# Cross attention's probabilities: two of four tiles turned by VectorE and through DRAM

## The chip, the cores and the metric

The kernel runs on one core of a Trainium2 chip. A core has a matrix engine, TensorE (PE in the profile; PEld is its weight load), and three others that compute: VectorE (DVE), ScalarE (ACT) and GpSimd (POOL). SyncE (SP) computes nothing; here it issues every DMA, in the order in which the program lists them, and when one has to wait, the ones behind it wait too. Each engine works through a list of its own, and semaphores make it wait for others. SBUF is the on-chip memory of 128 partitions, PSUM the eight banks into which TensorE writes, DRAM the large memory outside. The metric is the device time of one execution in microseconds. Lower is better.

## The reference

An encoder and a decoder layer of a transformer, in float32. The source has 2 x 77 tokens, the target 2 x 2048, the model 512 features, 16 heads of 32, and a feed-forward width of 2048. The part in question is the decoder's cross attention, then its feed-forward:

```python
def _mha(xq, xkv, w_in, b_in, w_out, b_out, bias):
    q = (xq @ wq.T + bq).reshape(Bq, Tq, H, hd).transpose(0, 2, 1, 3)
    ...
    scores = jnp.einsum('bhqd,bhkd->bhqk', q, k) / jnp.sqrt(hd) + bias[None]
    attn = jax.nn.softmax(scores, axis=-1)
    out = jnp.einsum('bhqk,bhkd->bhqd', attn, v).transpose(0, 2, 1, 3).reshape(Bq, Tq, D)
    return out @ w_out.T + b_out
...
y = y + _mha(yn, yn, ..., sb)                      # self attention, causal
y = y + _mha(_ln(y, ...), memory, ..., cb)         # cross attention: 77 keys
h = _ln(y, ...)
y = y + (jax.nn.relu(h @ dec_ff1_w.T + dec_ff1_b) @ dec_ff2_w.T + dec_ff2_b)
```

The bias depends on the distance of key and query, cut off at 127; against 77 keys it differs from head to head by a constant only from the third tile of 128 queries on, which the softmax does not see. So only the first two tiles of each batch have a bias added.

## The kernel before

The target is cut into 8 blocks of 512 tokens (2 batches of 4), a block into 4 tiles of 128 tokens. The first part of the program, up to about 1665 us, is self attention, with the encoder and the first block's cross attention woven in. The second part runs the feed-forward of block x and, between its matmuls, the cross attention of block x + 1, so seven times in all.

A block of the second part has 56 slots. Slots 0 to 27 each run one product of the first feed-forward matmul (L1636), slots 28 to 55 two products of the second (L1665; every fourth slot has one). Both are done by a scheme that multiplies seven products of halves instead of eight, so partial sums stay in a PSUM bank and go on being added to after an engine has read them: a bank that has been read late holds up a matmul four slots on. The stages of cross attention are functions which a table puts into slots; in a slot they are issued first, then the slot's own products, then the DMAs of the next weight tiles (`feed`, L1548). For tile t the table was: scores at slot 13 + 5t, and the others 2, 3, 3, 7 and 11 slots on.

The stages of one tile:

- **score**: 16 products of a head's queries with the 77 keys (L822; the queries lie in a buffer called `bias`, the keys in `pts`), into four banks. VectorE adds the bias where there is one (L829), takes each row's maximum (L831) and subtracts it on the way into SBUF (L832). The destination `pr` has 16 x 77 columns; tiles 0 and 2 use a part of the tile named `oT`, tiles 1 and 3 a part of `pts`.
- **exp**: ScalarE, one instruction over `pr` (L835).
- **sums**: VectorE sums each head's row and takes the reciprocal (L840, L841).
- **normalize**: GpSimd multiplies `pr` by it (L846).
- **turned**: TensorE turns each head's 128 x 77 into 77 x 128, four heads to a bank, and ScalarE copies each bank to `pts` (L852, L853).
- **times_v**: 16 products with v, four heads beside one another on the array (L860), and a copy by ScalarE (L864).

After each second tile come the out-projection's products (L1799, added by VectorE at L1803) in `O_SLOTS`, slots 31 to 34 and 40 to 43, and then each tile's normalization for the feed-forward (L779 to L800). Evictions of the first feed-forward matmul are L1646, L1649 and L1652, those of the second L1673 to L1685; the sums of halves that it needs are L1585, L1603 and L948.

Weight tiles of 256 KB come through a ring of 16 in `pp`. When a slot's products are done with a tile, SP loads the tile that will be used 16 tiles later into its place. Residual rows (`vv<-y`, L1359) and output rows (L1693) go through the same SP queue. A DMA on this queue uses one of eight semaphores in turn.

## Time and profile before

| | |
|---|---|
| time, median of 3 runs | 2706.46 us (2704.81 to 2711.2) |
| the profiled execution | 2708.39 us, its span 2706.3 us, granted clock 0.998 |
| PE, PEld, DVE, ACT, POOL busy | 99%, 81%, 68%, 56%, 37% of the span |
| second part, 1670 to 2606 us: PE, DVE, ACT, POOL busy | 936.0, 530.1, 388.8, 520.7 us of 936 |
| DMA in that stretch | 0.65 of the 16 engines, 195 GB/s |

Times are in us from the start of the span, unless marked ns. A group's row reads: line, engine, operation, output<-inputs with shapes, count | busy time, mean ns of one | idle time of the engine just before them and what ended it. A row of the chain of waits has start, length, and what ran. A row of a timeline has start, length, engine, line and instruction. A float32 product shows as two rows on PE, a turn as one: 16 products with v are "x32", 16 turns "x16".

### The profile page before, as it was taken

Reading aid. Unit: us, or ns where it says so; the run is one execution under the profiler, and the core shown is the slowest. Engines: PE = TensorE matmul, PEld = TensorE weight load, DVE = VectorE, ACT = ScalarE, POOL = GpSimd, SP = SyncE. Lnnn points to the kernel's source line nnn. Section 1 sums busy time; section 2 is a strip of 40 time slices with the busy share of each in tenths; the row PEclk is TensorE's granted clock in tenths of the full one; section 3 lists DMA queues with packets and bytes.
Section 4 is the critical chain, followed back from the end, with each engine's and each line's share of the span. In section 5 each row is a group of like instructions: output and inputs, shape, how many; then the busy total and the mean of one; then the engine's idle time right before and its main releaser. Section 6 shows DMA issues by size and latency. Waiting matters only on the chain.

```text
span 2706.3 us, 68257 instructions
## 1 busy us (share of the span) xinstructions
PE 2684.3 (99%) x26606; PEld 2199.2 (81%) x26606; DVE 1848.9 (68%) x5448; ACT 1526.2 (56%) x2960; POOL 1002.3 (37%) x844
## 2 busy tenths in 40 slices
PE   9999999999999999999999999999999999999998
PEld 6678777777776677778777887999999898989898
DVE  4776688888885687788888883737464746464635
ACT  3545567767886557777767794444443444444431
POOL 2602235500300513223300103556565555556546
PEclk9999999999999999999999999999999999999999
DMA  8734445511213522343311216565658565657575
GB/s 235 215 99 131 128 146 174 169 59 43 64 49 87 144 80 81 111 126 118 107 53 40 73 59 196 176 211 172 215 169 241 172 215 171 215 170 216 153 222 186
DMA packets 296276, 385.10 MB, mean 142 GB/s; under 512 B 41184, under 2 KB 165648, under 8 KB 295826
## 3 DMA queue, kind: packets, MB, share of 16 engines
q1 hardware_dynamic: 295954, 380.73, 46.9%
q8 instruction: 211, 3.46, 0.5%
q14 instruction: 111, 0.91, 0.1%
HBM read 334.15 MB, written 46.47 MB: 141 GB/s over the span
## 4 chain that ended last, share of the span: by engine, by line
PE 96%; DVE 1%; ACT 1%; DMA 1%; POOL 1%; SPq 0%; issue 0%; DVEq 0%; POOLq 0%; ACTq 0%
PE psum L417 18%; PE psum L1636 15%; PE psum L1665 13%; PE psum L375 11%; PE psum L441 9%; PE psum L1120 8%; PE psum L1799 3%; PE psum L1756 3%; PE psum L1035 3%; PE psum L852 2%; PE psum L822 1%; PE psum L860 1%; PE psum L576 1%; PE psum L797 1%; PE psum L239 1%; PE psum L215 1%
## 5 line engine op out<-in xcount | busy, mean ns | idle before, releaser
L406 ACT ACTIVATE pp<-pp,nm 128x128 f32<-128x128 f32 (+15 forms) x512 | 611.4, 1200 | 23.4 <-DVE nm L401 23.2
L384 DVE TENSOR_SCALAR_CACHE_REDUCE pp<-psum 128x512 f32<-128x512 f32 (+3 forms) x1024 | 556.7, 590 | 69.2 <-PE psum L375 67.1
L423 ACT COPY pts<-psum 128x512 f32<-128x512 f32 x696 | 374.4, 593 | 346.3 <-PE psum L417 309.5
L417 PE MATMUL psum<-ident,pp 128*128 128x128 f32 x4352 | 527.4, 276 | 5.7 <-ACT nT L310 4.0
L417 PEld LDWEIGHTS psum<-ident,pp 128*128 128x128 f32 x4352 | 475.2, 141 | 64.5 <-issue 21.4
L441 PEld LDWEIGHTS psum<-pts,vv 128*32 128x32 f32 x8704 | 225.7, 110 | 119.4 <-DVE pp L384 49.3
L375 PE MATMUL psum<-kT,q 32*128 32x512 f32 (+3 forms) x2560 | 320.3, 565 | 2.2 <-ACT kT L231 1.4
L421 DVE COPY pts<-psum 128x512 f32<-128x512 f32 x392 | 257.7, 686 | 84.8 <-PE psum L417 81.3
L1665 PE MATMUL psum<-pp 128*128 128x128 f32 x2560 | 304.5, 276 | 1.9 <-POOL pp L948 1.6
L1665 PEld LDWEIGHTS psum<-pp 128*128 128x128 f32 x2560 | 296.3, 192 | 8.6 <-issue 2.8
L441 PE MATMUL psum<-pts,vv 128*32 128x128 f32 x8704 | 278.0, 275 | 1.1 <-DVE pp L384 0.8
L948 POOL TENSOR_TENSOR pp<-pp 128x512 f32<-128x512 f32 x159 | 212.8, 1355 | 110.2 <-ACT pp L800 45.4
L1636 PE MATMUL psum<-vv,pp 128*128 128x256 f32 x1024 | 236.2, 381 | 0.0
L1636 PEld LDWEIGHTS psum<-vv,pp 128*128 128x128 f32 x1024 | 190.3, 190 | 25.8 <-issue 0.5
L391 DVE CUSTOM_DVE_ANT_0 pp<-psum,bias 128x256 f32<-128x256 f32 (+1 forms) x512 | 196.0, 411 | 13.2 <-PE psum L375 12.7
L375 PEld LDWEIGHTS psum<-kT,q 32*128 32x128 f32 x2560 | 127.5, 183 | 87.3 <-issue 50.0
L1649 DVE TENSOR_TENSOR kT<-kT,psum 128x512 f32<-128x512 f32 x96 | 65.8, 686 | 191.1 <-PE psum L1636 190.9
L1652 ACT ACTIVATE kT<-kT,vecs 128x256 f32<-128x256 f32 x192 | 86.9, 501 | 156.6 <-DVE kT L1649 155.9
L1636 PE MATMUL psum<-nT,pp 128*128 128x256 f32 x768 | 174.1, 380 | 0.0
L1636 PEld LDWEIGHTS psum<-nT,pp 128*128 128x128 f32 x768 | 144.2, 190 | 20.3 <-issue 1.6
L1673 ACT COPY oT<-psum 128x128 f32<-128x128 f32 x56 | 15.0, 268 | 239.1 <-PE psum L1665 239.1
L480 POOL TENSOR_TENSOR oT<-rirows,oT 128x512 f32<-128x512 f32 x30 | 38.4, 1279 | 288.6 <-DMA rirows<-rec 267.0
(272 smaller groups left out, 4108.2 us busy)
## 6 DMA issues: line engine op xcount, KB each, us to landing
pp<-w_d SPq DMA_DIRECT2D x520, 256.0 KB
pp<-in_dec_ff_wT_dram SPq DMA_DIRECT2D x112, 256.0 KB
bias<-tzg SPq DMA_DIRECT2D x128, 128.0 KB
pp<-wo_d SPq DMA_DIRECT2D x56, 256.0 KB
wqk<-in_dec_sa_in_wT_dram SPq DMA_DIRECT2D x52, 256.0 KB
wqk<-sa_q SPq DMA_DIRECT2D x84, 128.0 KB
vv<-in_enc_ff_wT_dram SPq DMA_DIRECT2D x8, 1024.0 KB
xr<-in_x_dram SPq DMA_DIRECT2D x32, 256.0 KB
```

Source lines behind the costliest of these rows:

```text
L375: nc.tensor.matmul(banks[r][:, : kn * P], q[rows4(r), ts(t, P)], kT[rows4(r), g, k0 * P : (k0 + kn) * P], start=True, stop=True,)
L384: nc.vector.tensor_scalar(p[:, k0 : k0 + far], s[:, :far], 1.0, None, ALU.mult, ALU.max, accum_out=st["mx"][:, r, c : c + 1],)
L391: nc.vector.tensor_tensor_reduce(p[:, k0 + far : i + 1], s[:, far:kn], near[:, 2 - (kn - far) :], 1.0, LOWEST, ALU.add, ALU.max, accum_out ...
L406: nc.scalar.activation(p, p, AF.Exp, bias=nm, accum_out=to)
L417: nc.tensor.transpose(pt[:, ts(x, P)], state[n]["p"][r][:, k], ident)
L421: nc.vector.tensor_copy(pts[:, : len(load), :], pt[:, :w])
L423: nc.scalar.copy(pts[:, : len(load), :], pt[:, :w])
L441: nc.tensor.matmul(ot[rows4(r)], vv[:, k, ts(g * HC + r, HD)], got.pop((n, k, r)), start=k == ks[0] and (whole or not begun), stop=k == ks ...
L948: engine.tensor_tensor(out, a, b, ALU.subtract)
L1120: nc.tensor.matmul(mm[:, ts(f, TOK)], left[:, c, ts(f, P)], right[:, c, :], start=c == 0, stop=c == 1,)
L1636: nc.tensor.matmul(mm[:, ts(f, TOK)], a[:, c, ts(f, P)], b[:, c, :], start=fresh and f == 0 and c == 0, stop=c == 1, skip_group_check=True,)
L1665: nc.tensor.matmul(psum[:, bank_i, ts(col, P)], lhs[:, c, :], w[:, c, :], start=fresh and k in (0, 3) and c == 0, stop=c == 3, skip_group_ ...
```

## The change

Tiles 1 and 3 of each block (`MOVED`) are no longer turned by TensorE. Their `pr` is laid out in three chunks of 32 keys, each with 16 heads x 32 columns, padded from 77 to 96 keys (the pad is set to zero once). VectorE turns it in place, in blocks of 32 x 32 (L899). One DMA writes it to a DRAM tensor `crossed` (L900, 128 x 3 x 512), and in a later slot (`BACK`) three DMAs read it back, 32 keys each, so that keys lie on partitions (L904), into `landing`. Products with v read it there, a head's 128 tokens as four runs of 32. For these tiles the subtraction, the exponential, the sums and the normalization are made in pieces, since the padded layout is not one row per head.

`landing` takes the last four places of the weight ring, which has 12 tiles then. New tables set the slots of all stages (`TILES`, `OUTS`, `NORMS`). The first block's cross attention in the first part stays as it was.

```diff
-        def attend_stages(q, kTc, v, y, biased, pr, pts, place, w_o, bi=None):
+        def chunked(pr):
+            c = pr.rearrange("p (c h x) -> p c h x", h=H, x=RB)
+            full = S // RB
+            return c[:, :full], c[:, full, :, : S - full * RB]
+
+        def attend_stages(q, kTc, v, y, biased, pr, pts, place, w_o, bi=None, bounce=None):
+            apart = bounce is not None
+            if apart:
+                full, rest = chunked(pr)
+                far = full.shape[1] * RB
...
                     nc.vector.tensor_reduce(mx[:, :, r], s, AX.X, ALU.max)
-                    nc.vector.tensor_tensor(d, s, mx[:, :, r, None].to_broadcast([P, NC, S]), ALU.subtract)
+                    m = mx[:, :, r, None].to_broadcast([P, NC, S])
+                    for d, ks in in_parts(r) if apart else ((d, slice(None)),):
+                        to = (split(s, ks), split(m, ks)) if apart else (s, m)
+                        nc.vector.tensor_tensor(d, *to, ALU.subtract)
 
             def exp():
-                nc.scalar.activation(pr, pr, AF.Exp)
+                for p in (full, rest) if apart else (prh,):
+                    nc.scalar.activation(p, p, AF.Exp)
...
+                if apart:
+                    nc.vector.tensor_reduce(su, full.rearrange("p c h x -> p h c x"), AX.XY, ALU.add)
+                    nc.vector.tensor_reduce(ri, rest, AX.X, ALU.add)
+                    nc.vector.tensor_tensor(su, su, ri, ALU.add)
...
+                    for c in range(n):
+                        nc.gpsimd.tensor_tensor(full[:, c], full[:, c], ri[:, :, None].to_broadcast([P, H, RB]), ALU.mult)
+                    nc.gpsimd.tensor_tensor(rest, rest, ri[:, :, None].to_broadcast([P, H, S - far]), ALU.mult)
...
+            def turned_out():
+                nc.vector.transpose(pr, pr)
+                nc.sync.dma_start(bounce.rearrange("c p x -> p c x"), pr.rearrange("p (c x) -> p c x", x=H * RB))
+
+            def moved():
+                for c in range(-(-S // RB)):
+                    nc.sync.dma_start(pts[ts(c, RB), :, :], bounce[c].rearrange("(a k) x -> k a x", k=RB))
...
+                        pT = pts[:S, :, ts(h, RB)] if apart else pts[:S, g, ts(r, P)]
                         nc.tensor.matmul(
-                            ot[rows4(r), ts(g, P)], v[:, ts(h, HD)], pts(g)[:, ts(r, P)], start=True, stop=True
+                            ot[rows4(r), ts(g, P)], v[:, ts(h, HD)], pT, start=True, stop=True
                         )
...
-        prs = [oflat[:, : H * S], pts_all[:, 5:8, :].rearrange("p a k -> p (a k)")[:, : H * S]]
+        PADDED = H * 3 * RB
+        prs = [oflat[:, :PADDED], pts_all[:, 5:8, :].rearrange("p a k -> p (a k)")]
+        landing = low[:, END // 2 - HC * D :].rearrange("p (a x) -> p a x", a=HC)
+        crossed = dram.tile([3, P, H * RB], F32, name="crossed", tag="crossed")
...
-        O_SLOTS = {at + k: js for at in (31, 40) for k, js in enumerate(((0, 1), (2, 3), (4, 5), (6,)))}
+        MOVED = (1, 3)
+        TILES = ((13, 14, 14, 16, 20, 26), (16, 16, 18, 20, 20, 28), (23, 24, 27, 27, 29, 33), (27, 28, 29, 29, 31, 39))
+        BACK = (22, 23, 32, 33)
+        OUTS = ((31, 32, 33, 34), (41, 43, 44, 45))
+        NORMS = ((44, 47, 49), (37, 38, 46), (46, 48, 53), (48, 49, 54))
+        O_SLOTS = {at[k]: js for at in OUTS for k, js in enumerate(((0, 1), (2, 3), (4, 5), (6,)))}
...
-        w_ring = [low[:, ts(j, D)] for j in range(16)]
+        w_ring = [low[:, ts(j, D)] for j in range(END // 2 // D - HC)]
...
-                    feed(turned_to[n])
+                    feed(min(turned_to[n], len(w_ring)))
...
+            if x == 1:
+                plan[7].append(lambda: [gp.memset(p[:, PADDED - H * RB :], 0.0) for p in prs])
...
-                for k, f in zip((0, 2, 3, 3, 7, 11), fs):
-                    plan[at + k].append(f)
+                for k, f in zip(TILES[t], fs[:6]):
+                    plan[k].append(f)
+                if moves:
+                    plan[BACK[t]].append(fs[6])
...
```

Where it moves instructions: three places, each in one of the later blocks. On PE, from tile 0's turns to tile 2's, before:

```order
L852 MATMUL psum<-ident,oT 77x128 x16
L1636 MATMUL psum<-vv,pp 128x256 x12
L822 MATMUL psum<-pts,bias 128x77 x16
L1636 MATMUL psum<-vv,pp 128x256 x4
L860 MATMUL psum<-pts,q 32x128 x16
L1636 MATMUL psum<-nT,pp 128x256 x4
L852 MATMUL psum<-ident,pts 77x128 x16
```

and with the change (line numbers are larger: L844 scores, L895 turns, L912 products with v, L1697 and L1726 the feed-forward):

```order
L895 MATMUL psum<-ident,oT 77x128 x16
L1697 MATMUL psum<-vv,pp 128x256 x12
L844 MATMUL psum<-pts,bias 128x77 x16
L1697 MATMUL psum<-vv,pp 128x256 x4
L1697 MATMUL psum<-nT,pp 128x256 x8
L912 MATMUL psum<-pts,q 32x128 x16
L1697 MATMUL psum<-vv,pp 128x256 x4
L844 MATMUL psum<-pts,bias 128x77 x16
L1697 MATMUL psum<-vv,pp 128x256 x4
L912 MATMUL psum<-pp,q 32x128 x16
L1726 MATMUL psum<-pp,kT 128x128 x8
L895 MATMUL psum<-ident,oT 77x128 x16
```

Tile 1's turns (the last row before) are gone. Its products with v now read `pp`, where `landing` is; they stand in slot 28, behind tile 3's scores, and stood in slot 29 before. On VectorE, from the end of tile 1's scores on, before:

```order
L832 TENSOR_TENSOR pts<-psum,cmx 128x4x77
L840 TENSOR_REDUCE csu<-pts 128x16
L841 RECIPROCAL cri<-csu 128x16
L1649 TENSOR_TENSOR kT<-kT,psum 128x2x256
L831 TENSOR_REDUCE cmx<-psum 128x4
```

and with the change:

```order
L863 TENSOR_TENSOR pts<-psum,cmx 128x4x2x32
L863 TENSOR_TENSOR pts<-psum,cmx 128x4x13
L1710 TENSOR_TENSOR kT<-kT,psum 128x2x256 x2
L873 TENSOR_REDUCE csu<-pts 128x16
L874 TENSOR_REDUCE cri<-pts 128x16
L875 TENSOR_TENSOR csu<-csu,cri 128x16
L878 RECIPROCAL cri<-csu 128x16
L899 STREAM_TRANSPOSE pts<-pts 128x1536
L1710 TENSOR_TENSOR kT<-kT,psum 128x2x256
L859 TENSOR_REDUCE cmx<-psum 128x4
```

The turn stands between tile 1's sums and the eviction of slot 22 (L1710), with tile 2's scores behind it; it waits for GpSimd's normalization. On SP the change puts four DMAs among the weight tiles for each moved tile:

```order
L900 DMA crossed<-pts 128x3x512
L1609 DMA pp<-w_d 128x512 x3
L904 DMA pp<-crossed 32x4x512 x3
L1609 DMA pp<-wo_d 128x512 x2
...
L900 DMA crossed<-pts 128x3x512
L1609 DMA pp<-w_d 128x512
L1415 DMA vv<-y_1_3_84 128x512
L1609 DMA pp<-w_d 128x512 x4
L904 DMA pp<-crossed 32x4x512 x3
L1609 DMA pp<-w_d 128x512 x8
```

The write waits for VectorE and the first read for the write, both at the head of SP's queue, with three weight tiles between them for tile 1, five and a residual row for tile 3.

More of the change, by code (lines that the diff above doesn't have):

```diff
@@ L870, in out @@
                 nc.vector.tensor_tensor(y(), mm, y(), ALU.add)
+            if apart:
+                return score, exp, sums, normalize, turned_out, times_v, moved, keep
             return score, exp, sums, normalize, turned, times_v, out, keep
@@ L894, in first_cross @@
             oT, xn = kT[:, 1, 3 * MB :], kT[:, 2, 3 * MB :]
[L896 to L897 removed]
+            pts = kT[:, :, 2 * MB : 3 * MB]
             def loads():
@@ L1820, in cross @@
                 bias_1 = [a[:, : NC * S].rearrange("p (g k) -> p g k", k=S) for a in spare]
-                plan[3].append(lambda: bias_tile(prs[0].rearrange("p (h k) -> p h k", k=S), 2, P, S, 255))
+                wide = prs[0].rearrange("p (c h x) -> p c h x", h=H, x=RB)
+                flat = prs[0][:, : H * S].rearrange("p (h k) -> p h k", k=S)
+                parts = [(wide[:, k // RB, :, : min(RB, S - k)], k) for k in range(0, S, RB)] if 0 in MOVED else [(flat, 0)]
+                plan[3].append(lambda: [bias_tile(d, 2, P, d.shape[2], 255, k0=k) for d, k in parts])
                 plan[5].append(lambda: [bias_tile(a, 2, P, S, 255 - P, r, HC) for r, a in enumerate(bias_1)])
             for t in range(TB):
-                at = 13 + 5 * t
                 y = lambda t=t: y_of(x, t)
                 biased = m == 0 and t < 2
+                moves = t in MOVED
                 fs = attend_stages(
-                    lambda g, t=t: qT[g // 2][:, g % 2, ts(t, P)], kTc, vc[0][:S, :], y, biased, prs[t % 2],
-                    lambda g: pts_all[:S, g, :], place("xr"), wbt,
-                    bias_1 if biased and t else None,
+                    lambda g, t=t: qT[g // 2][:, g % 2, ts(t, P)], kTc, vc[0][:S, :], y, biased,
+                    prs[t % 2] if moves else prs[t % 2][:, : H * S], landing if moves else pts_all[:, :HC, :],
+                    place("xr"), wbt, bias_1 if biased and t else None, crossed if moves else None,
                 )
```

54 lines of the change are left out of this document (35 added, 19 removed).

## The prediction

> **What bounds the kernel now.** I read the page first: the engines' busy shares and the chain that ended last.
>
> ```profile
> span 2706.3 us, 68257 instructions
> PE 2684.3 (99%) x26606; PEld 2199.2 (81%) x26606; DVE 1848.9 (68%) x5448; ACT 1526.2 (56%) x2960; POOL 1002.3 (37%) x844
> PE 96%; DVE 1%; ACT 1%; DMA 1%; POOL 1%; SPq 0%; issue 0%; DVEq 0%; POOLq 0%; ACTq 0%
> ```
>
> TensorE (PE) is busy for 99% of the span and makes 96% of the chain. A busy PE need not be one that cannot go faster, so I looked next at the stretch that the change touches (windows; the columns are PE, PEld, DVE, ACT, POOL, granted clock, DMA share, GB/s), and at what PE waits for from 1520 us on.
>
> ```profile
> 1670.00:2606.00 936.00, 935.97 (x7447) 851.22 (x7447) 530.05 (x1033) 388.78 (x827) 520.68 (x444) 1.00 0.65 195
> PE psum L1665 <- POOL pp L948: 1.6, 2, 1.2
> PE psum L1665 <- DVE pp L948: 0.3, 1, 0.3
> PE psum L441 <- DVE pts L421: 0.2, 1, 0.2
> ```
>
> For 936 us PE has no gap, at full clock, and in the whole second half it waits 2.1 us in all. So the stretch lasts as long as PE's list of matmuls, and what leaves that list leaves the time, until something arrives late. That list, for one block (the chain of waits over 2194 to 2328 us):
>
> ```profile
> 2231.38 1.06 PE psum L822 x32
> 2232.44 8.83 PE psum L1636 x40
> 2241.27 1.06 PE psum L822 x32
> ...
> 2247.73 5.18 PE psum L1636 x24
> ...
> 2255.89 1.01 PE psum L860 x32
> 2256.91 1.92 PE psum L1636 x8
> 2258.83 1.75 PE psum L852 x16
> ...
> 2266.82 1.98 PE psum L1665 x16
> ...
> 2273.69 1.79 PE psum L1665 x16
> 2275.48 1.73 PE psum L1799 x8
> ...
> 2288.99 1.75 PE psum L852 x16
> ```
>
> L822 is one tile's scores (1.06), L852 its 16 turns (1.75), L860 its 16 products with v (1.01). One slot of the first feed-forward product is 8 rows of L1636 (5.18 / 3 = 1.73); a slot of the second is 16 rows of L1665 (1.79), every fourth 8 rows (0.89); two out-products are 8 rows of L1799 (1.73). These are the ruler for everything below.
>
> **What is removed.** Tiles 1 and 3 of each of seven blocks no longer run L852: 14 tiles, 14 x 1.75 = 24.5 us of PE, taken start to start in the chain.
>
> ```profile
> L852 PE MATMUL psum<-ident,pts 128*77 128x128 f32 x224 | 26.7, 273 | 0.0
> L853 ACT COPY pts<-psum 77x512 f32<-77x512 f32 x112 | 56.9, 586 | 20.4 <-PE psum L852 20.4
> ```
>
> The group itself says 26.7 us (overlaps with the next matmul counted); that is the upper end. Half of the 112 copies go as well, 33 us of ScalarE: nothing on the path, since ScalarE is busy 389 of the 936 us. PE gets nothing new: the products with v keep their count, but read their moving operand as four runs of 32 columns, not one of 128. No row shows such an operand; between nothing and a doubling (14 x 1.01 = 14 us) I take nothing, as L1636 and L1665 already run on views in pieces on their other operand.
>
> **What is added**, all beside PE: VectorE subtracts in two pieces, reduces in two, and turns 128x1536; GpSimd normalizes in three instructions, ScalarE exponentiates in two; SP writes 786 KB (128 x 1536 x 4) to DRAM and reads it back in three DMAs. Hidden, if the turned tile is in its place when PE reaches its products with v. So the sum is a race of two clocks for each moved tile. The prices:
>
> ```profile
> L831 DVE TENSOR_REDUCE cmx<-psum 128x4 f32<-128x308 f32 x112 | 52.9, 472 | 33.6 <-PE psum L822 33.6
> L832 DVE TENSOR_TENSOR pts<-psum,cmx 128x308 f32<-128x308 f32 x52 | 24.9, 479 | 2.3
> L1649 DVE TENSOR_TENSOR kT<-kT,psum 128x512 f32<-128x512 f32 x96 | 65.8, 686 | 191.1 <-PE psum L1636 190.9
> L840 DVE TENSOR_REDUCE csu<-pts 128x16 f32<-128x1232 f32 x14 | 20.0, 1432 | 23.4 <-ACT pts L835 23.4
> L841 DVE RECIPROCAL cri<-csu 128x16 f32<-128x16 f32 x32 | 8.1, 253 | 1.1
> L835 ACT ACTIVATE pts<-pts 128x1232 f32<-128x1232 f32 x14 | 17.4, 1241 | 0.0
> L846 POOL TENSOR_TENSOR pts<-pts,cri 128x1232 f32<-128x1232 f32 x14 | 31.5, 2250 | 59.0 <-DVE cri L841 59.0
> L470 DVE STREAM_TRANSPOSE rt<-ri 128x32 f32<-128x32 f32 x30 | 6.4, 212 | 1.0
> L781 DVE TENSOR_SCALAR crs<-cmv 128x1 f32<-128x1 f32 x64 | 9.8, 154 | 2.2
> L1803 DVE TENSOR_TENSOR vv<-vv,psum 128x256 f32<-128x256 f32 x98 | 39.6, 416 | 33.8 <-PE psum L1799 32.5
> 2239.34 0.25 DVE L841 RECIPROCAL cri<-csu 128x16 f32<-128x16 f32 x1
> 918.00 1.57 SPq L262 DMA_DIRECT2D xr<-in_x_dram  x2
> 920.96 1.27 POOL L1090 TENSOR_TENSOR xr<-xr,row_dec_sa_out_b 128x512 f32<-128x512 f32 x1 [5.00 <-DMA xr<-in_x_dram]
> 2313.00:2320.00 7.00, 7.00 (x65) 7.00 (x64) 5.51 (x15) 2.91 (x6) 5.95 (x8) 1.00 0.91 288
> ```
>
> The turn is the unknown one. Below, 1.8 us: 1536 columns at the rate of L840 (1.17 ns). Above, 48 times the 32-column row: 10.2 us. By that same row less a one-column instruction (212 - 154 = 58 ns), 154 + 48 x 58 = 2.9 us, which I take, since it is the operation itself. A DMA: a 262 KB row asked for at 918.00 is used at 920.96, so 2.1 us beside 0.9 of transfer at 288 GB/s; 786 KB is then 2.1 + 2.7 = 4.8 us, each way.
>
> [...]
>
> **Tile 1** is scored in slot 16 and multiplied in slot 28. On PE lie between: 12 slots of 1.73, two more scores and its own (3 x 1.06), the turns of tile 0 (1.75) and its products (1.01), and about 0.1 at each switch: 27.3 us from the start of its scores. The other clock, with the same zero: VectorE is first done with tile 0 at 2239.6 - 2231.4 = 8.2 after slot 13 starts, which is 1.9 (slot 16 starts 6.3 later); maxima and subtractions 4 x (0.47 + 0.6) to 6.2; two L1649 to 7.6, the exponential (1.24, in two perhaps 1.5) beside them to 7.8; sums 1.43 + 0.25 and two small ones, to 10.0; GpSimd 2.25 as one, about 3.2 as three, to 13.2; turn to 16.1; write landed 20.9; read landed 25.7, or 26.4 if the three weight tiles between the two go first (2.1 + 2.36 MB / 288). It is 0.9 to 1.6 us early.
>
> **Tile 3** is turned by VectorE behind the two adds (L1803) of the out-products of slot 31, and multiplied in slot 39. From the end of those products PE has 0.89, 1.73 + 1.79, 1.73 + 1.01 + 1.98, 0.87 + 1.79, 0.89 and 3 x 1.79: 18.1 us. The other clock: 0.4 add, 2.9 turn, to 3.3; then in one queue the write, five weight tiles, a row of y and the read, 3.14 MB: 2.1 + 10.9, to 16.3. 1.8 us early. With no company it would be 12.9.
>
> **Behind the waiting instructions.** VectorE stands at L899 for GpSimd: behind it are the eviction of slot 22 (due before slot 26, as the bank is added to again there) and tile 2's scores. Turn 1 ends at 16.1, slot 22's product at about 15.1 and slot 26 starts at 22.6, so 5 us of room. SP stands at the write from slot 19's tile on, some 8 us, and at the read for the landing; weight tiles queue behind it. These are the rows for SP before:
>
> ```profile
> SPq L1548 <- PE psum L1636: 335.7, 212, 3.3
> SPq L1548 <- PE psum L1665: 271.8, 355, 2.7
> ```
>
> SP waits for PE to free a tile, not for DMA, so the ring is always full. With 12 tiles and 7 used per 6.26 us in the second product, the lead is 10.7 us (it was 14.3); a tile needs 3.0. The blocks of SP fit, with little over. In bytes: 936 x 195 = 182.5 MB plus 14 x 1.57 = 22 over 911 us is 224 GB/s, under the 288 that a window reaches. The block whose tiles 0 and 1 get a bias has 4 x 0.48 us more on VectorE for each: once, about 1 us late.
>
> **Sum.** The profiled execution took 2708.4 (span 2706.3 and 2.1 around it), 0.07% over the median 2706.5 of the runs. 2708.4 - 24.5 + 1 = 2684.9, by the median **2683**; own range 2677 (26.7 gained and a little) to 2690.
>
> **Rivals.**
> 1. The round trip comes late: both slacks are under 2 us, and are made of estimates. Let each transfer take 1.3 to 1.8 us more, both 2.6 to 3.6, and take the slack of some 1.6 off: each tile is 1 to 2 us late, 14 to 28 us go back, 2696 to 2710, and nearer the first. For it: 0.91 DMA share in some windows; against: 0.65 on average.
> 2. Slower: the turn costs what 48 small ones cost, 10.2 us, 7.3 over mine. Tile 1 is then 6.0 late, tile 3 5.5, as its turn starts from slot 31 anew: 7 x 11.5 - 24.5 = +56, 2763. It decides from a turn of about 6 us on (1.75 late per tile eats the gain). For it: the only row of this instruction; against: 154 of its 212 ns are what one column costs.
> 3. The moving operand in four runs doubles L860: 2683 + 14 = 2697.
> 4. The change does not do what it says, since weights, not matmuls, set the pace with 12 tiles: no gain, 2706. Against it: the wait rows of SP. [...] PEld is 851 of 936 here, and PE does not wait.
>
> **Chances.** Forecast 0.66, late 0.16, slower 0.08, operand 0.05, no gain 0.05. Range 2676 to 2701, which holds the first, most of rival 1, and rival 3. Changes within 0.3% (8 us) count as none: faster takes 0.66 + 0.05 and 0.10 of rival 1; same the other 0.06 and rival 4; slower rival 2 and a bit.
>
> **What will show it.** L895, the turns left, at 224 in the second half and L912 still 1.01 a tile; PE's waits at L912 for a DMA from crossed: none or tenths if right, 1 to 2 us each by rival 1, 5 to 6 by rival 2; L899 at 1.8 to 2.9 us; no PE wait on w_d. Wrong outright if PE's busy time falls by 24 us and the span does not.

## The result, and the profile after

The changed kernel takes **2693.03 us** (median of five runs, 2692.04 to 2697.57) against 2708.02 for the kernel before beside it (2704.81 to 2711.20): a ratio of 0.9947, 95% interval 0.9933 to 0.9962. That is 15.0 us less, where 23.5 were forecast. The time lies inside the range and beyond the 0.3%, on the side of faster; the forecast of 2683 is 10 too low.

The page's first lines after, and the two lines of shares of its chain of waits:

```profile
span 2695.8 us, 67958 instructions
PE 2664.8 (99%) x26382; PEld 2178.2 (81%) x26382; DVE 1886.1 (70%) x5546; ACT 1497.3 (56%) x2918; POOL 998.2 (37%) x874
PE 90%; DMA 4%; DVE 2%; ACT 1%; POOL 1%; SPq 1%; issue 1%; DVEq 0%; POOLq 0%; ACTq 0%
```

PE is busy 19.5 us less (2684.3 before), the span only 10.5 less, and the chain now has 4% of DMA where it had 1%. The groups that the change made or touched (the columns are busy time, mean ns of one, and the idle time ahead of them):

```profile
L895 PE MATMUL psum<-ident,oT 128*77 128x128 f32 x224 | 27.0, 273 | 0.0
L912 PE MATMUL psum<-pts,q 77*32 77x128 f32 x448 | 15.1, 276 | 0.0
L912 PE MATMUL psum<-pp,q 77*32 77x128 f32 x448 | 15.1, 276 | 0.1
L899 DVE STREAM_TRANSPOSE pts<-pts 128x1536 f32<-128x1536 f32 x14 | 24.8, 1774 | 19.1 <-POOL pts L887 19.1
L886 POOL TENSOR_TENSOR pts<-pts,cri 128x512 f32<-128x512 f32 x28 | 33.7, 1224 | 17.4 <-ACT kT L1713 7.9 <-DVE cri L878 4.6 <-issue 4.1
L887 POOL TENSOR_TENSOR pts<-pts,cri 128x208 f32<-128x208 f32 x14 | 7.7, 551 | 0.0
```

The change did what it says: 224 turns are left. The products with v cost the same whether their moving operand lies in one run (from `pts`) or in four (from `pp`): 15.1 us for 448 of each, and those of the moved tiles wait 0.1 us in all. The turn takes 1.77 us.

What PE waits for from 1520 us on (us in total, times, longest), and below it what SP waits for at the new lines:

```profile
PE psum L1726 <- DMA pp<-w_d: 7.1, 5, 1.7
PE psum L1726 <- POOL pp L1001: 1.6, 2, 1.2
PE psum L1726 <- POOL crs L782: 1.4, 1, 1.4
PE psum L844 <- ACT xr L916: 0.7, 1, 0.7
```

```profile
SPq L900 <- DVE pts L899: 33.8, 7, 8.5
SPq L900 <- DVE oT L1740: 23.0, 7, 3.8
SPq L904 <- DMA crossed<-pts: 14.0, 11, 1.7
SPq L1609 <- DMA pp<-w_d: 33.1, 69, 1.8
```

The first and third row of PE are one place: a matmul of slot 38 (L1726 is what L1665 was), the last ahead of tile 3's products, waits for its weights in six of the seven blocks (the row that names POOL too: GpSimd had long been done). The chain of waits over 2262 to 2295 us shows what came before:

```profile
2272.75 0.44 SPq L1609
2273.19 0.05 issue
2273.24 6.38 DMA vv<-y
...
2279.68 9.07 DMA pp<-w_d
2288.76 0.14 issue
2288.89 1.13 PE psum L1726 x8
2290.02 1.01 PE psum L912 x32
```

SP asks for that weight tile at 2279.68, once a row of y asked for at 2273.24 has landed (the eight semaphores go round, and this DMA takes that of the row, eight DMAs earlier), and the tile needs 9.07 us to land. Around it, as issue time, tile, and time until all of it has landed, from the records of the DMAs:

```
2272.29 L900  crossed<-pts  4.43      2276.78 L904  pp<-crossed   8.88
2272.75 L1609 pp<-w_d       4.66      2277.15 L904  pp<-crossed   9.91
2273.24 L1415 vv<-y         6.38      2278.29 L904  pp<-crossed  10.03
2274.32 L1609 pp<-w_d       6.03      2279.68 L1609 pp<-w_d       9.07
...                                   2280.41 L1609 pp<-w_d       9.03
```

Everything is slow while the read back (L904) runs. These windows show that it is not the bytes (the last two columns are DMA share and GB/s):

```profile
1670.00:2596.00 926.00, 916.58 (x7234) 830.98 (x7233) 569.16 (x1133) 359.94 (x785) 517.90 (x474) 1.00 0.74 222
2281.00:2285.00 4.00, 4.00 (x38) 4.00 (x38) 2.43 (x6) 0.00 (x0) 2.29 (x2) 1.00 1.08 192
2285.00:2289.00 4.00, 2.36 (x22) 2.19 (x21) 3.93 (x7) 0.27 (x1) 3.21 (x4) 1.00 1.04 250
```

From 2281 on the DMA engines are full, and move 192 GB/s. Elsewhere in the same program a full stretch moves nearly twice that, as the durations of the 2 KB packets show, in ns (5th, 25th, 50th, 75th, 95th percentile; the read back runs from 2281 to 2288):

```
2278 to 2280 us   84  84  84  84 116   361 GB/s
2282 to 2284 us  144 151 156 168 218   205 GB/s
2284 to 2286 us  146 158 171 195 247   190 GB/s
2286 to 2288 us   89 114 153 197 225   220 GB/s
2288 to 2290 us   84  84  84  86  93   370 GB/s
```

**A better ruler.** The whole time varies by several us between runs of one kernel, and the profiles show one place where it does: ahead of the first product of q (L1756 before, L1817 after), where no tile is moved. The rows of that line, with its first and last start, in the kernel before and in the changed one:

```profile
L1756 PE MATMUL psum<-pp x392: 379/379/379, 1664.0 to 2503.3; 128*128 128x256 f32 x196
L1817 PE MATMUL psum<-pp x392: 379/379/379, 1665.8 to 2494.6; 128*128 128x256 f32 x196
```

In the 14 profiles of this study that first start lies between 1660.0 and 1666.4 us, with no order by kernel. It goes with the granted clock, the share of its full clock that TensorE is given, which ahead of it falls to 0.5 for 3.4 us at a time: once in five profiles (first start 1660.0 to 1661.2), four times in three others (1664.7 to 1666.4). From there to the end of the span the kernel before takes 2706.3 - 1664.0 = **1042.3** and the changed one 2695.8 - 1665.8 = **1030.0**. With only its ring of weight tiles cut, the kernel before takes 1042.3 again (first experiment), so tenths count here, as long as the clock stays whole behind the mark (1.00 in these three profiles). Each kernel has one profile. Below, "the stretch" is this time, and the change is worth 12.3 us of it; the other 2.7 of the 15.0 fall in the spread ahead of it.

### The profile page after: what moved, and what is told of

Read it like the earlier page. It is cut to its first block, busy times and chain, and to the rows that moved or that the text cites. A ratio compares the mean times of both kernels' runs of the same rounds, so it can differ in the third digit from the quotient of the medians.

```text
span 2695.8 us, 67958 instructions
## 1 busy us (share of the span) xinstructions
PE 2664.8 (99%) x26382; PEld 2178.2 (81%) x26382; DVE 1886.1 (70%) x5546; ACT 1497.3 (56%) x2918; POOL 998.2 (37%) x874
## 4 chain that ended last, share of the span: by engine, by line
PE 90%; DMA 4%; DVE 2%; ACT 1%; POOL 1%; SPq 1%; issue 1%; DVEq 0%; POOLq 0%; ACTq 0%
PE psum L417 18%; PE psum L1697 14%; PE psum L1726 11%; PE psum L375 10%; PE psum L441 9%; PE psum L1173 8%; PE psum L1817 3%; PE psum L1862 3%; PE psum L1088 3%; DMA pp<-w_d 2%; PE psum L844 1%; PE psum L895 1%; PE psum L797 1%; PE psum L912 1%; PE psum L576 1%; PE psum L215 1%
## 5 line engine op out<-in xcount | busy, mean ns | idle before, releaser
L1726 PE MATMUL psum<-pp 128*128 128x128 f32 x2560 | 305.4, 276 | 10.4 <-DMA pp<-w_d 7.1
L1726 PEld LDWEIGHTS psum<-pp 128*128 128x128 f32 x2560 | 297.4, 192 | 17.2 <-POOL crs L782 8.7
L1001 POOL TENSOR_TENSOR pp<-pp 128x512 f32<-128x512 f32 x159 | 204.3, 1305 | 112.1 <-DMA pp<-in_dec_ff_wT_dram 49.5
L1697 PE MATMUL psum<-vv,pp 128*128 128x256 f32 x1024 | 238.1, 382 | 0.0
L1697 PEld LDWEIGHTS psum<-vv,pp 128*128 128x128 f32 x1024 | 189.7, 190 | 27.0 <-issue 1.7
L1710 DVE TENSOR_TENSOR kT<-kT,psum 128x512 f32<-128x512 f32 x96 | 64.5, 685 | 167.7 <-PE psum L1697 167.7
L1697 PE MATMUL psum<-nT,pp 128*128 128x256 f32 x768 | 174.1, 380 | 0.0
L1713 ACT ACTIVATE kT<-kT,vecs 128x256 f32<-128x256 f32 x192 | 85.3, 498 | 137.0 <-DVE kT L1710 136.3
L1697 PEld LDWEIGHTS psum<-nT,pp 128*128 128x128 f32 x768 | 144.7, 190 | 19.8 <-issue 0.2
```

Source lines behind the costliest of these rows:

```text
L1001: engine.tensor_tensor(out, a, b, ALU.subtract)
L1697: nc.tensor.matmul(mm[:, ts(f, TOK)], a[:, c, ts(f, P)], b[:, c, :], start=fresh and f == 0 and c == 0, stop=c == 1, skip_group_check=True,)
L1726: nc.tensor.matmul(psum[:, bank_i, ts(col, P)], lhs[:, c, :], w[:, c, :], start=fresh and k in (0, 3) and c == 0, stop=c == 3, skip_group_ ...
```

## The experiments

Four theories on the missing 9 to 12 us. **R**: the ring of 12 tiles is too small by itself. **Q**: SP, standing at L900 and L904, asks for the weights too late. **V**: the bytes of the round trip alone fill the DMA engines. **P**: the read back is slow for where it lands, 32 partitions at a time, and holds up the weights behind it.

**Ring alone.** In the kernel before:

```diff
-        w_ring = [low[:, ts(j, D)] for j in range(16)]
+        w_ring = [low[:, ts(j, D)] for j in range(12)]
...
-                    feed(turned_to[n])
+                    feed(min(turned_to[n], len(w_ring)))
```

> Edit to the kernel before: its ring has 12 weight tiles instead of 16 and nothing else changes. It separates the smaller ring from the moved tiles. Theories P and Q: without a round trip the lead of 10.7 us is enough, 2706 to 2709, no PE wait on w_d over 0.5 us. Rival R (ring): the 9 us that are missing from the gain are the price of four tiles fewer: 2713 to 2717.

Measured: 2705.34 us, ratio 0.9998 (0.9990 to 1.0007); stretch 1042.3, no wait on w_d. R falls: by itself the smaller ring costs nothing. Whether a ring of 16 would have absorbed the delays of the moved tiles is not tested.

**Tile 1 alone, tile 3 alone.** In the changed kernel:

```diff
-        MOVED = (1, 3)
-        TILES = ((13, 14, 14, 16, 20, 26), (16, 16, 18, 20, 20, 28), (23, 24, 27, 27, 29, 33), (27, 28, 29, 29, 31, 39))
+        MOVED = (1,)
+        TILES = ((13, 14, 14, 16, 20, 26), (16, 16, 18, 20, 20, 28), (23, 24, 27, 27, 29, 33), (27, 28, 29, 29, 35, 39))
```

> Edit to the changed kernel: only tile 1 is moved, tile 3 is turned by TensorE as before (in slot 35, its slot of before). Theories P, Q and V, in which the loss is all at the weight tile ahead of tile 3's products: the seven tiles pay in full, 7 x 1.75 = 12.3 us, no wait on w_d: 2708.0 - 12.3 = 2695.8 (2694 to 2698), so that tile 3 brings only some 3 us. If the loss is spread over both tiles: half of the measured gain, 2708 - 7.5 = 2700.5 (2699 to 2702).

```diff
-        MOVED = (1, 3)
-        TILES = ((13, 14, 14, 16, 20, 26), (16, 16, 18, 20, 20, 28), (23, 24, 27, 27, 29, 33), (27, 28, 29, 29, 31, 39))
+        MOVED = (3,)
+        TILES = ((13, 14, 14, 16, 20, 24), (16, 16, 18, 20, 25, 28), (23, 24, 27, 27, 29, 33), (27, 28, 29, 29, 31, 39))
```

> Edit to the changed kernel: only tile 3 is moved, tile 1 is turned by TensorE in slot 25 and tile 0 multiplied in slot 24, as before the change. From the first q product to the end (before 1042.3, both tiles 1030.0, tile 1 alone 1034.9): if tile 3's round trip makes all of the late weight tiles, they are late here too, some 1.4 us in each of six blocks, and the gain is what both bring less what tile 1 alone brings, 4.9: 1037.4 (1036.5 to 1038.5). If the late tiles need both round trips, they are gone and the gain is 7 x 1.5 = 10 or so: 1031 to 1033.

Measured: tile 1 alone 2697.88 us, ratio 0.9971 (0.9960 to 0.9982), stretch 1034.9, no wait on w_d. Tile 3 alone 2703.07, ratio 0.9989 (0.9980 to 0.9998), stretch 1037.2, and this row:

```profile
PE psum L1726 <- DMA pp<-w_d: 3.2, 3, 1.8
```

Tile 1 brings 7.4, tile 3 5.1, and 7.4 + 5.1 = 12.5 is near what both bring together (12.3). Tile 3's round trip makes the weights late even alone. But the waits are not those foretold: 3.2 us in three blocks, where both tiles have 8.5 in six, and some 1.4 in each of six was expected here too. So the time came as expected and its parts did not, and that the two sums are so near is not shown to mean more. Tile 1, with no weights late, brings 7.4 and not the 12.3 expected: its blocks take 135.7 us instead of 137.0, so 1.3 a tile and 0.1 in the block with the biases. Of that loss its wait rows show 1.1 us, once in each block:

```profile
PE psum L1862 <- DVE vv L1866: 1.1, 7, 0.2
```

The table of PE's time further down shows the rest.

**Rows of y earlier.** In the changed kernel:

```diff
-            if FIRST <= n < FIRST + TB:
-                new_y(x + 2, n - FIRST)
+            if 22 <= n < 22 + TB:
+                new_y(x + 2, n - 22)
```

> Edit to the changed kernel: the four rows of y of the block after next, 1.05 MB, are loaded beside slots 22 to 25 instead of 28 to 31, so they no longer run into the read back of tile 3. Theory P: 1.05 MB less at the slow rate, or at least 3 us less in front of the late tile (by the window 2281 to 2289 at some 200 GB/s up to 5 us); the waits of 1.7 us go or nearly go: 2685 to 2688. Theory V says the same, 2685 to 2687. Theory Q: the y rows are four instructions of SP, of 0.4 us each, in front of L900: 2690 to 2693.

Measured: 2689.27 us, ratio 0.9935 (0.9922 to 0.9947); stretch 2684.6 - 1661.1 = 1023.5. PE's waits:

```profile
PE psum L1726 <- POOL pp L1001: 1.6, 2, 1.2
PE psum L912 <- DVE pts L863: 1.0, 1, 1.0
PE psum L1862 <- DVE vv L1866: 0.8, 5, 0.2
PE psum L844 <- ACT xr L916: 0.7, 1, 0.7
```

```profile
SPq L900 <- DVE pts L899: 33.8, 7, 8.5
SPq L900 <- DVE oT L1740: 26.5, 7, 3.8
SPq L904 <- DMA crossed<-pts: 15.6, 14, 1.7
```

The whole time lies between the ranges that were foretold (to 2688 by P and V, from 2690 by Q); the waits decide. No wait on w_d is left, and the stretch is 6.5 shorter, while SP stands at L900 and L904 no less than in the changed kernel (33.8, 26.5 and 15.6 against 33.8, 23.0 and 14.0). That speaks against Q, and the read into 128 partitions below settles it. P and V both foretold that the waits go.

**Read back into 96 partitions, asked for by groups of queries.** In the changed kernel:

```diff
-                for c in range(-(-S // RB)):
-                    nc.sync.dma_start(pts[ts(c, RB), :, :], bounce[c].rearrange("(a k) x -> k a x", k=RB))
+                for a in range(P // RB):
+                    nc.sync.dma_start(pts[: 3 * RB, a, :], bounce[:, ts(a, RB), :])
```

> Edit to the changed kernel: the read back is asked for as four DMAs of 96 partitions (one for each group of 32 queries) instead of three DMAs of 32 partitions (one for each chunk of keys); the bytes and the place are the same. Theory P (partitions): in the changed kernel 2 KB packets take 84 ns, but 151 to 171 ns (median) while a read back into 32 partitions runs, so the DMA engines are full at 190 to 220 GB/s and the weight tile of slot 38 comes up to 1.7 us late, 7.1 + 1.4 us in six blocks. With 96 partitions the packets stay near 84 ns, the waits of PE at L1726 for w_d go to under 1 us in all: 2693.0 - 8 = 2685 (2683 to 2687). Theory Q (queue): SP stands at L900 and L904 and asks for the weight tiles too late, whatever the rate: no change, 2692 to 2694. Theory V (volume): the bytes alone fill the engines; no change either, 2692 to 2694.

Measured: 2810.62 us, ratio 1.0388 (1.0373 to 1.0402), stretch 1146.6, with these waits, and the window of its stretch (the clock is the third number from the end):

```profile
PE psum L1726 <- DMA pp<-w_d: 50.1, 7, 7.5
PE psum L912 <- DMA pp<-crossed: 29.3, 6, 7.6
1661.50:2808.10 1146.60, 1054.60 (x7865) 957.74 (x7863) 605.45 (x1198) 383.81 (x840) 574.95 (x514) 0.94 0.65 197
```

No theory expected this. The records of a read show that it lands in another way than the rest: the semaphore rises in 4 steps, the first 1.1 us after the issue and the last up to 15.2 us after it, where the write and the weight tiles show 16 steps. Unlike those, these reads have a source whose slowest dimension is 3 (the chunks). That this makes the 4 steps was the author's reading; no run changes it alone. So this run tells nothing of P.

It shows another cost, though. The waits are not all of the 116.6 us that it loses against the changed kernel: with each of its 14 waits of 4.1 to 7.6 us, beginning within it or at most 0.5 us behind it, comes a time of 3.4 to 13.7 us in which the granted clock is 0.5, and over the stretch the clock is 0.94, where the changed kernel has 1.00.

**Write by groups of queries, read back as one DMA of 96 partitions.** This keeps 96 as the slowest dimension of the read:

```diff
-                nc.sync.dma_start(bounce.rearrange("c p x -> p c x"), pr.rearrange("p (c x) -> p c x", x=H * RB))
+                for a in range(P // RB):
+                    nc.sync.dma_start(
+                        bounce[a].rearrange("(c k) x -> k c x", k=RB), pr[ts(a, RB)].rearrange("p (c x) -> p c x", x=H * RB)
+                    )
...
-                for c in range(-(-S // RB)):
-                    nc.sync.dma_start(pts[ts(c, RB), :, :], bounce[c].rearrange("(a k) x -> k a x", k=RB))
+                nc.sync.dma_start(pts[: 3 * RB], bounce.rearrange("a p x -> p a x"))
...
-        crossed = dram.tile([3, P, H * RB], F32, name="crossed", tag="crossed")
+        crossed = dram.tile([P // RB, 3 * RB, H * RB], F32, name="crossed", tag="crossed")
```

> Edit to the changed kernel: the probabilities go to DRAM in four writes of 32 partitions (one for each group of queries), laid down so that the read back is one DMA of 96 partitions, whose outermost dimension on both sides is 96. The bytes are the same. [...] Theory P (a transfer that touches 32 partitions at a time is slow, 151 to 171 ns a packet): the read runs at 84 ns a packet and is there 3.5 to 5 us after it is asked for (it was 5 to 11), the slow packets move to the writes, which land 5 to 7 us after the issue instead of 4.3; the write of tile 3 lies further ahead of the weight tile that was late, so the waits at L1726 for w_d fall under 3 us: from the first q product to the end 1023.5 to 1027 us (changed kernel 1030.0). Theory V (bytes alone): packets as slow as before, same waits, 1029 to 1031. If only landing in 32 partitions is slow and leaving from 32 is not, the writes stay at 4.3 us and the waits go altogether: 1023 to 1024.

Measured: 2700.11 us, ratio 0.9980 (0.9967 to 0.9993), stretch 1033.7.

```profile
PE psum L1728 <- DMA pp<-w_d: 6.5, 5, 1.6
PE psum L1728 <- POOL crs L783: 2.0, 1, 2.0
```

The read has 16 steps, but lands 6 to 10.5 us after its issue, at 158 to 159 ns a packet (median, 2286 to 2290 us). The writes, now leaving from 32 partitions each, run at some 150 ns from their start (medians 146 to 151), where the changed kernel's write, at 1704.35, has some 235 of its 384 packets at 84 to 88 ns and the last 145 or so at 154. All but three of the 56 writes still land within 3.6 us of their issue (the three within 4.9), and the last of four in most cases 4.9 after the first is asked for. So the expectation failed in its middle: 96 partitions did not make the read fast. Of the 1033.7, about 3.4 us are the clock: behind the wait of 2.0 us in the second row it is 0.5 for 6.8 us, and that block takes 139.0 where the five others take 134.7 to 137.4. Without that the stretch would be an estimated 1030, where theory V had it. Three kinds of transfer were slow by now (medians of 146 to 171 ns a packet), into 32, out of 32, and into 96, and fast (84 to 88 ns) were reads into 128 and the larger part of the write from 128. That left V and a cause on DRAM's side open.

**Both edits together.**

> Both edits to the changed kernel: the split write with one read of 96 partitions, and the rows of y loaded beside slots 22 to 25. The early rows alone leave no wait on w_d, so the faster read has nothing left to save at that place by any of the theories: 1023 to 1024 us from the first q product to the end, the same as with the early rows alone (1023.5). If it is under 1022.5, transfers delay PE in ways that its waits do not show; if over 1025, the four writes of 32 partitions cost something of their own.

Measured: 2696.11 us, ratio 0.9962 (0.9950 to 0.9974), stretch 1031.2, 7.7 more than with the early rows alone.

```profile
PE psum L914 <- DMA pp<-crossed: 5.2, 3, 2.4
PE psum L1728 <- DMA pp<-w_d: 3.9, 4, 1.5
```

It is the case "over 1025", and now the round trip itself is late too (L914 is the products with v). Whether that comes from the four writes or from the one read into 96 partitions, which lands 7.4 to 11.0 us after its issue here, this run does not part.

**The same read into 128 partitions.** This tells P from V: same bytes, same source, same moment, another landing, which leaves the probabilities in the wrong place.

```diff
-                    nc.sync.dma_start(pts[ts(c, RB), :, :], bounce[c].rearrange("(a k) x -> k a x", k=RB))
+                    nc.sync.dma_start(pts[:, c, :], bounce[c])
```

> Edit to the changed kernel: the read back is three DMAs of 128 partitions, each one chunk as it lies in DRAM, so the same 786 KB are read from the same place at the same moment, but land with each row on the partition of its number; this leaves out the right place of the probabilities (the products with v then use others), not any instruction. Landing in 32 partitions (changed kernel) and in 96 (split write) both ran at 150 to 171 ns a packet, and so did leaving from 32 (147 to 149); only transfers of 128 partitions ran at 84. Theory P in its new form (the rate hangs on how many partitions of SBUF a transfer has, 128 for the full one): packets at 84 to 90 ns during the read, landed 4 to 5 us after it is asked for, waits at L1726 for w_d under 1 us in all, 1023 to 1024.5 us from the first q product to the end. Theory D (the DRAM side: data just written, or the strides of the read): still 150 ns and more, waits of 5 us or more, 1028 to 1031. Theory V (bytes alone): the engines stay full, as the bytes do not change; waits of 5 us or more.

Measured: 2686.44 us, ratio 0.9926 (0.9912 to 0.9941), stretch 2683.5 - 1661.0 = 1022.5. The stretch of its read and the one behind it (it asks for the write at 2263.9, the changed kernel at 2272.3), and PE's longest waits:

```profile
2273.00:2277.00 4.00, 4.00 (x38) 4.00 (x37) 2.54 (x5) 0.00 (x0) 2.68 (x2) 1.00 1.06 396
2277.00:2281.00 4.00, 4.00 (x59) 3.68 (x58) 3.61 (x7) 0.42 (x2) 3.21 (x5) 1.00 1.05 384
```

```profile
PE psum L1726 <- POOL pp L1001: 1.6, 2, 1.2
PE psum L1862 <- DVE vv L1866: 1.2, 7, 0.2
PE psum L844 <- ACT xr L916: 0.7, 1, 0.7
```

The engines are as full (1.06 against 1.08) and move 396 GB/s instead of 192; the packets take 84 ns (median, 2271 to 2275 us), and no wait on w_d is left, though tile 3's reads land 5.1 to 7.3 us after their issue, not 4 to 5. V falls. Q falls too: the weight tile that was late is asked for 7.6 us behind the write here and 7.4 in the changed kernel, and lands 5.3 us later instead of 9.1. Of DRAM's side, the data just written falls. The order of the rows does not: they are read one after another here, and 32 apart in the changed kernel, so this run changes the order together with the landing. The simplest reading is that it is how the transfer lies on the partitions of SBUF; the order in DRAM stays as a rival. In GB/s, the core's DMAs move 190 to 220 while the read lands in 32 partitions, 384 to 396 while it lands in 128, and 216 to 234 in the run with the split write, where it lands in 96. Why 96 partitions bring so little more than 32 is open, and so is what in the hardware makes the difference.

**Three tiles.** With the rows of y out of the way there is room, so tile 0 was moved too:

```diff
-        MOVED = (1, 3)
+        MOVED = (0, 1, 3)
-        TILES = ((13, 14, 14, 16, 20, 26), (16, 16, 18, 20, 20, 28), (23, 24, 27, 27, 29, 33), (27, 28, 29, 29, 31, 39))
-        BACK = (22, 23, 32, 33)
-        OUTS = ((31, 32, 33, 34), (41, 43, 44, 45))
+        TILES = ((13, 14, 14, 16, 17, 25), (16, 16, 18, 20, 20, 30), (23, 24, 27, 27, 29, 33), (27, 28, 29, 29, 31, 39))
+        BACK = (19, 26, 32, 33)
+        OUTS = ((33, 34, 35, 36), (41, 43, 44, 45))
```

> A try for a faster kernel: the changed kernel with the rows of y beside slots 22 to 25, and tile 0 moved as well (turn in slot 17, read back in slot 19, products in slot 25; tile 1's read back behind them in slot 26, its products in slot 30, the out-products of tiles 0 and 1 in slots 33 to 36). Seven more tiles at 1.5 us each, as one tile has paid so far: 1023.5 - 10 = 1013 us from the first q product to the end, if the three round trips fit. If tile 0's read, which now has about 8 us from the end of the turn, or the weight tiles behind it come late by 1 us or more in each block, 1018 to 1030; the block with the biases gains least.

Measured: 2721.04 us, ratio 1.0057 (1.0042 to 1.0071), stretch 1059.1. Its wait, and one of its places:

```profile
PE psum L912 <- DMA pp<-crossed: 33.6, 8, 5.8
2000.66 1.75 PE L912 MATMUL psum<-pp,q 77*32 77x128 f32 x32 [4.24 <-DMA pp<-crossed]
2000.90:2004.30 3.40, 3.40 (x41) 3.02 (x33) 1.19 (x4) 0.59 (x1) 0.27 (x1) 0.50 0.55 202
```

That is tile 1: its read back was asked for at 1990.35 to 1991.81, behind the four rows of y (1985.96 to 1989.05), and landed at 2000.4. Tile 0 made PE wait in the block with the biases only. The wait is paid twice: in the 3.4 us of the last row, a window, the granted clock is 0.50 (third number from the end), and the 16 products take 1.75 us where they take 1.08 in the last block. This follows each of the six waits of over 4 us here. The edit that had helped two tiles stood in the way of the third. So the rows went to slots 42 to 45:

```diff
-            if 22 <= n < 22 + TB:
-                new_y(x + 2, n - 22)
+            if 42 <= n < 42 + TB:
+                new_y(x + 2, n - 42)
```

> The kernel with three moved tiles, with one edit: the rows of y are loaded beside slots 42 to 45 instead of 22 to 25. In the run before, tile 0 cost PE no wait, but the read back of tile 1 was asked for at 1990.4 behind four rows of y (issued 1986.0 to 1989.1) and landed 8 to 9 us later, 4.2 us after PE wanted it (1996.4); periods were 140. If the rows are what makes it late (1.05 MB at some 200 to 390 GB/s is 2.7 to 5 us): the wait at L912 falls to 0 to 1.5 us in each block, periods 132.5 to 134, 1013 to 1022 us from the first q product to the end. If it is late by itself (its own 786 KB at 200 GB/s and the weights of the second product): wait still over 3 us, periods over 136, 1035 or more. Rows of y in slots 42 to 45 may make weight tiles late there instead: a wait at L1726 for w_d of up to 1 us in each block.

and then, in a second run, the products of tile 1 to slot 31 as well:

```diff
-        TILES = ((13, 14, 14, 16, 17, 25), (16, 16, 18, 20, 20, 30), (23, 24, 27, 27, 29, 33), (27, 28, 29, 29, 31, 39))
-        OUTS = ((33, 34, 35, 36), (41, 43, 44, 45))
-        NORMS = ((44, 47, 49), (37, 38, 46), (46, 48, 53), (48, 49, 54))
+        TILES = ((13, 14, 14, 16, 17, 25), (16, 16, 18, 20, 20, 31), (23, 24, 27, 27, 29, 33), (27, 28, 29, 29, 31, 39))
+        OUTS = ((34, 35, 36, 37), (41, 43, 44, 45))
+        NORMS = ((44, 47, 49), (38, 39, 46), (46, 48, 53), (48, 49, 54))
```

> As the run above, and the products of tile 1 in slot 31 instead of 30, the out-products of tiles 0 and 1 in slots 34 to 37, so that tile 1's read has 1.8 us more. If the round trip is then in time in every block, the wait at L912 is gone: periods 132.5, 1012 to 1015 us from the first q product to the end, 2675 us or so in all. If the later out-products make tiles 2 and 3 or the norms wait, a new wait stands at L895, L912 or L1862, and the gain is less: 1016 to 1025.

Measured: with the rows moved 2684.21 us, ratio 0.9923 (0.9910 to 0.9936), stretch 1017.6, 3.6 us of wait left at L912; with slot 31 as well 2679.61, ratio 0.9906 (0.9891 to 0.9921), stretch 1015.7, periods of 131.9 to 132.2 in five of the six blocks that a next one follows, and 140.0 in the one with the biases.

In that block alone tile 0 was then left on TensorE:

```diff
-                parts = [(wide[:, k // RB, :, : min(RB, S - k)], k) for k in range(0, S, RB)] if 0 in MOVED else [(flat, 0)]
+                parts = [(wide[:, k // RB, :, : min(RB, S - k)], k) for k in range(0, S, RB)] if False else [(flat, 0)]
...
-                moves = t in MOVED
+                moves = t in MOVED and not (biased and t == 0)
...
-                for k, f in zip(TILES[t], fs[:6]):
+                for k, f in zip(TILES[t] if moves or t else (13, 14, 14, 16, 20, 25), fs[:6]):
```

> The kernel of the run above (three tiles, rows of y beside slots 42 to 45, tile 1 in slot 31), with one edit: in the block whose tiles 0 and 1 get a bias, tile 0 stays on TensorE. There the period was 140.0 against 132.0 elsewhere, with 2.65 us of wait at L912 for tile 0's read, 1.43 at L1697 for VectorE and 1.15 at L844. If the moved tile 0 is what that block can't hold: its period falls to 134 to 136.5 (it was 136.4 with tiles 1 and 3 moved), 1010 to 1012.5 us from the first q product to the end, and 2674 to 2676 in all. If the loss lies with the biased tile 1 and the later slots, the period stays at 138 to 140 and the time at 2679.

Measured: **2675.27 us**, ratio 0.9886 (0.9869 to 0.9902), stretch 2675.7 - 1664.7 = 1011.0; that block takes 134.3. Its waits from 1520 us on:

```profile
PE psum L912 <- DMA pp<-crossed: 2.3, 4, 0.8
PE psum L1726 <- POOL pp L1001: 1.6, 2, 1.2
```

It beats both kernels: 31.3 us less than before in the stretch, 19.0 less than the changed kernel.

## Why the prediction was right in sign and too high in gain

PE's time in one block of the second part, from each matmul's start to the next one's, summed by the function that issued it. The block is the second (its wait for weights is one of the short ones: four of the others have 45.9 to 46.1 at second_product in the changed kernel); behind it, the one with the biases:

```
                  before   changed   y earlier  |  with biases: before  changed  y earlier
turned             10.78      7.04       7.04   |               11.04     7.40      7.41
times_v             4.04      4.04       4.04   |                4.04     4.04      4.04
score               4.24      4.47       4.47   |                4.24     5.38      5.39
first_product      49.38     49.58      49.57   |               49.38    49.85     50.73
second_product     44.26     45.01      44.47   |               44.26    46.08     44.47
o_product          12.20     12.20      12.30   |               12.20    12.20     12.30
q_product          12.08     12.09      12.09   |               12.09    12.09     12.08
```

- **What is removed** (24.5, at most 26.7): 10.78 - 7.04 = 3.74 a block, 7 x 3.74 = 26.2. Right, and nearer the upper end: beside 2 x 1.75 a block, a short wait of 0.15 in one group of turns and 0.09 between turns and products with v are gone as well.
- **What it costs PE elsewhere** was in the sum as nothing. It is 0.23 (scores) + 0.19 (first product) + 0.21 (second) + 0.10 (out-products) = 0.73 a block, 5.1 in seven. It is not that PE changes more often from one kind of matmul to another: it does so 62 times in this block before and 60 times with the early rows. The starts of the matmuls show three places. Tile 3's scores wait 0.22 us for ScalarE's copy of products with v (L916), in pieces too short for a row of waits. One more group of scores or of products with v stands inside the first feed-forward product, where such a group costs 0.09 ahead of it and 0.10 behind. And one pair of out-products waits for VectorE (the row of L1862 on L1866) and loses 0.4 in all. Some 0.1 is saved elsewhere. Tile 1 alone, with no weights late, has the same 0.73, which is why it paid 1.3 a tile.
- **The block with the biases**, "once, about 1 us late": with the early rows it takes 136.4 against 134.0 in the others, from 137.2 and 137.0 before, so 2.2 less gain. The size was off by a factor of two.
- **The read back, 4.8 us, and "the blocks of SP fit, with little over"**: this is the step that failed. The write was right (4.2 to 4.9 us). The read took 5.8 to 7.8 us for tile 1 and 9.6 to 11.5 for tile 3, as 288 GB/s was taken from a window of other transfers, and the reads into 32 partitions ran at 190 to 220. What came late was not the tile but the weights behind it. Price: 1030.0 - 1023.5 = 6.5 us.

Together: 26.2 - 5.1 - 2.2 - 6.5 = 12.4, against 12.3 measured.

The other steps. The turn was priced at 2.9 (1.8 to 10.2) and takes 1.77: the lower bound was the answer, 1.16 ns a column, and rival 2 (10.2) is out. That gave the round trip 1.1 us that the slow read then took. The moving operand in four runs costs nothing (276 ns a row either way), so rival 3 is out. The ring of 12 is harmless by itself, as predicted; rival 4 is out. The bytes came to 222 GB/s (224 predicted).

**Rival 1** had the price right (both transfers 2.6 to 3.6 us more; tile 3's write and read, with their company, take 3.0 more in the block shown) and the place wrong. It put the wait at L912, and there 0.1 us was seen. But it was close: in the block shown, tile 3's read lands 17.8 us after its turn starts, and its products begin at 19.5, of which 1.6 are the wait for the weights. Without that wait the tile would have been just in time; its slack of 1.8 was gone. The result lies between the forecast and this rival.

Of the signs named, three came (224 turns, L912 at 1.01 a tile, no wait there for the crossed tiles beyond 0.1), L899 fell just under its bounds, and "no PE wait on w_d" was wrong. It was the one that showed the failed step.

## What to carry to other kernels

Price a transfer by the partitions it touches and not only by its bytes (a 2 KB packet took 84 ns in the reads into 128 here, medians of 146 to 171 into 32 or 96 and out of 32): a row of the same shape, or a window in which the DMA engines are full and the GB/s are low, gives the rate. When a transfer gets a new neighbour in a queue that already runs near its limit, look for what is asked for after it, since the wait shows there; here moving four unrelated loads out of the way was worth 6.5 us, and with them moved once more a third tile could move. Count a long wait of TensorE for more than its length, and read the granted clock behind it (it was 0.5 for at least 3.4 us with each wait of over 4 us here). Where runs of one kernel differ by several us, time the stretch that the edit touches from a mark inside the program.

## What the runs showed of the hardware

- The 32x32 turn of VectorE took 1774 ns for 128x1536 in float32, 1.16 ns a column, the rate of the sums over a row (L840, 1432 ns for 1232 columns) and a fraction of what 48 turns of 32 columns at 212 ns would add up to.
- 2 KB packets took 84 ns when a read landed in 128 partitions, and 146 to 171 ns (medians) when a transfer landed in 32 or in 96, or left from 32. The engines showed as full in the reads either way (1.04 to 1.08). In the write from 128 partitions some 235 of 384 packets took 84 to 88 ns and the last 145 or so 154; why is not shown.
- TensorE's granted clock was 0.5 for 3.4 to 13.7 us with each of the 20 waits of 4.1 to 7.6 us that PE has in the second part of these runs, beginning within the wait or just behind it. Of 21 waits of 1.2 to 2.7 us, 3 had such a time behind them.
- The reads whose source had a slowest dimension of 3 raised their semaphore in 4 steps, where the other DMAs looked at show 16, and took up to 15.2 us for 196 KB; why is not shown.
- The products with v whose moving operand came in four runs of 32 float32 columns took the same 276 ns as those with one run of 128.
